# The last stage of tiles 0 to 11 beside the last expert blocks of layer 1, in a two-layer graph-attention and mixture-of-experts kernel

## The chip, the cores and the metric

The kernel runs on one core of one Trainium2 chip. Times are device microseconds (us) of one execution. A profile records one further execution: its span runs from the first to the last recorded instruction of the program.

## What is computed

Two layers over 2708 tokens of 256 float32 numbers, each layer a graph attention and a mixture of experts with two experts per token. The part that the change touches is the end of layer 1:

```python
x = x + _L1_gnn_ref(_layernorm(x), adj, 1, ...)        # attention; its result is the x below
x = x + _L1_ffn_ref(_layernorm(x), gate_w, ..., gamma, beta)

def _L1_ffn_ref(x, gate_w, gate_b, w1, b1, w2, b2, gamma, beta):   # x: (2708, 256), E = 16, K = 2
    topk_vals, topk_idx = jax.lax.top_k(x @ gate_w + gate_b, K)
    topk_w = jax.nn.softmax(topk_vals, axis=-1)
    h = jax.nn.relu(jnp.einsum('bsh,ehf->bsef', x, w1) + b1)
    expert_out = jnp.einsum('bsef,efh->bseh', h, w2) + b2
    sel = jnp.take_along_axis(expert_out, topk_idx[:, :, :, None], axis=2)
    y = x + jnp.sum(topk_w[..., None] * sel, axis=2)
    mu, var = jnp.mean(y, axis=-1, keepdims=True), jnp.var(y, axis=-1, keepdims=True)
    return (y - mu) / jnp.sqrt(var + EPS) * gamma + beta
```

For every token, y is the normalised row plus two weighted expert outputs. y is normalised once more, scaled by gamma, shifted by beta, and added to the residual x.

## The kernel before

Tokens lie in 22 tiles: 20 of 128 rows and two of 74 (`TAIL`). The attention of layer 1 hands over groups of six tiles (the last of four). For each group a router picks two experts per token and writes the token's row twice into a DRAM table, `rows_d`, ordered so that each 128 rows (a block) belong to one expert. Blocks are made known in three stages: blocks 0 to 7 after 12 tiles, 8 to 19 after 18 tiles, the rest after all. 45 blocks always run (`SURE1`); more run only if a number read at run time says so (`rest`, L926 to L929, which every engine passes).

`Experts.stream` runs the blocks. For block b:

- SP fetches the block's 128 rows (`fetch`, L759), and loads the expert's weights w1 (`load_w1`, L743) and w2 (`load_w2`, L747), 512 KB each, into one of three rooms. Each weight load carries a condition: it is skipped when block b - 3, which used the same room, had the same expert.
- PE turns the rows (L455), ACT copies them (L992). PE computes the hidden layer in four pieces (L874), ACT applies the relu (L878), PE the outputs (L889, L892).
- DVE makes `side` (L866), ACT from it the weight w (L868), DVE finishes w (L896) and scales the outputs into `yo` (L898, four buffers).
- POOL issues an indirect DMA that adds the 128 rows of `yo` to one of two DRAM tables, `sums1[b % 2]` (`add`, L903). Two adds to the same table wait for each other's landing; `sums1[0]` also holds the normalised rows, so that the two tables together give y.

The outputs of block b - 1 come behind the hidden layer of block b on PE.

PE, ACT, DVE and SP run their instructions in the order in which the program issues them. That order is made by a planner, `Clock`: every piece of work is a generator that names an engine and a planned time, or waits for a mark; the planner resumes whichever is due first, and the instructions are issued then. A hidden piece is planned at 0.47 us, a turn at 0.4, a block's outputs at 2.05, handing over between engines at 0.25, a fetch at 0.5 us of DMA and 2.2 of latency, each weight load at 1.7 and 2.0. Lower `urgency` numbers go first. The order of POOL's instructions is not written by hand: whatever is ready in the build's own plan is placed first. Each engine, SP's queue of DMAs included, takes its instructions strictly in order.

Beside the stream, `add_beta(b)` is called once for every block. From block 22 on it issues two POOL operations for one tile (L1854, L1855), which turn x1, the residual, into x1 + common + beta.

After the stream comes the last stage, `last1`, for all 22 tiles in groups of 2, 2, 4, 4, 4, 4, 2 (`firsts`). `load_y` issues two loads per group, one from each table, into `y_all` (L1444, L1447; `y_all` lies in memory that held the attention mask). For each pair of tiles PE adds the two tables' rows into a PSUM bank, by multiplying with the identity (L1894), and DVE takes the statistics (L421, L422). For each group ACT computes the reciprocal root (L428, L429), DVE mends it by one Newton step and makes the shift (L374). Then ACT scales the rows (L446), POOL multiplies by gamma (L1914), DVE adds x1 (L1918, L1924) and SP stores pairs of tiles (L1920, L1926). The loads must wait until all 45 adds have landed; they follow on POOL a closing step of the conditional part.

Of the kernel before, what the change touches and what calls it, by code (L numbers as in the profile page):

```python
# [17 lines left out]
OP = mybir.AluOpType  # L18
# [4 lines left out]
P = 128  # L23
# [123 lines left out]
def kernel(  # L147
# [559 lines left out]
    class Experts:  # L707
# [5 lines left out]
        def __init__(self, layer, router, w1, b1, w2, func, sums, tags, xg, xt, bias, sure):  # L713
            self.layer, self.router, self.w1, self.w2 = layer, router, w1, w2
            self.func, self.sums, self.b1 = func, sums, b1
            self.t_tag, self.h_tag, self.o_tag = tags
            self.xg_tile, self.xt_tile, self.bias_tile = xg, xt, bias
            E, _, self.F = w1.shape
            self.FC, self.NB = self.F // P, router.blocks
            self.rooms, self.rows, self.known, self.planned, self.stages = {}, {}, 0, 0, []  # L720
            self.last_add, self.adds = {}, []
            self.b1_rows = w1x.rearrange("p c f -> p (c f)")[:E, :self.F]
            self.taken, self.sure = taken_of[layer], sure

# [176 lines left out]
        def add(self, b, yo):  # L901
            k = b % 2
            ins = nc.gpsimd.indirect_dma_start(  # L903
                out=self.sums[k][:, :], in_=yo, in_offset=None,
                out_offset=bass.IndirectOffsetOnAxis(ap=self.rows.pop(b)[:, D:D + 1].bitcast(I32),
                                                     axis=0), compute_op=OP.add)
            if k in self.last_add:
                tc.add_manual_dep(ins.ins, self.last_add[k].name, LANDED, reason="the same rows")
            self.last_add[k] = ins.ins
            if k == 0:  # L910
                self.adds.append(ins.ins)

        def outputs(self, b, ht, w):
            ps = ps_tile("out_ps", self.o_tag)
# [3 lines left out]
        def store(self, t, r, src):  # L918

            ins = nc.sync.dma_start(self.sums[0][t * P:t * P + r, :], src)  # L920
            for other in self.adds:
                tc.declare_no_dep(ins.ins, other, reason="other tokens' rows")

        def rest(self):

# [10 lines left out]
        def stream(self, clock, stages, bank, acc, xrs, los, wides, widened, started):  # L936

            NB, FC = self.sure, self.FC
            self.known_at, self.planned_at, self.scattered_at = (
                {upto: Mark() for upto in stages} for _ in range(3))  # L940
            hidden_at, out_at, xg_at, xt_at, ht_at, w_at = (
                [Mark() for _ in range(NB)] for _ in range(6))
            xr_slots, xts, weights, hidden = {}, {}, {}, {}
# [5 lines left out]
            def fetcher():  # L949
                for b in range(NB):  # L950
# [4 lines left out]
                    xr_slots[b] = yield from xrs.get()  # L955
                    self.fetch(b)
                    clock.moved(xg_at[b], 0.5, 2.2)

            def loader():
                yield widened  # L960
                for b in range(NB):
# [14 lines left out]
                        yield out_at[b - 3]  # L976
                    self.load_w2(b)
                    clock.moved(w_at[b], 1.7, 2.0)

            def turn(b):  # L980
                yield xg_at[b]
# [27 lines left out]
            def finish(b, ps, slot):  # L1009
                yield "DVE", 0.7  # L1010
                yo = self.scaled(b, ps, weights.pop(b))
                clock.set(slot)
                yield "POOL", 1.6
                self.add(b, yo)
                clock.set(xr_slots.pop(b))

            def outputs(b):
                slot = yield from acc.get()
# [420 lines left out]
    def fetch_rows(tl, src, group):  # L1439

        full = [t for t, r in group if r == P]
        if full:
            lo = full[0] * P
            nc.sync.dma_start(tl[:, :len(full)], src[lo:lo + len(full) * P, :].rearrange(  # L1444
                "(t p) d -> p t d", p=P))
        if len(full) < len(group):
            nc.sync.dma_start(tl[:TAIL, len(full):], src[TF * P:W, :].rearrange(  # L1447
                "(t p) d -> p t d", p=P)[:TAIL])

    x_d = dram.tile([W, D], F32, name="x_d")  # L1450

# [394 lines left out]
        experts1.add_room(2, room[:, :1024], room[:, 1024:])  # L1846

    def add_beta(b):
        if b == 20:
            for name, src in (("gamma", L1_ffn_gamma), ("beta", L1_ffn_beta)):  # L1850
                last[name] = broadcast_rows(name, src, 0, D, nc.sync, last["pool"])
        if 22 <= b < 22 + T:
            t, r = tiles[b - 22]
            nc.gpsimd.tensor_scalar(x1[:r, t, :], x1[:r, t, :], common[:r, t:t + 1], None, op0=OP.add)  # L1854
            nc.gpsimd.tensor_tensor(x1[:r, t, :], x1[:r, t, :], last["beta"][:r], OP.add)  # L1855

    experts1.beside = add_beta
    for t in range(2):
        clock.start(finish1(*tiles[t]), 0)
    clock.start(widener())  # L1860
    clock.start(attention(), 2)
    experts1.stream(clock, (*early1.values(), experts1.NB), bank, acc, xrs, los, wides, widened,
                    started)
    clock.run()
    experts1.rest()
    experts1_scope.close()

    psum_stage(wide=5, acc=3)

    y_all = mask_flat.bitcast(F32)[:, :2 * T * D].rearrange(  # L1870
        "p (k t d) -> p k t d", k=2, d=D)
    clock = Clock()
    bank = Slots(clock, 5)

    def load_y(group, mark):
        lo = group[0][0]
# [34 lines left out]
    def out_rows(pair):  # L1911
# [9 lines left out]
        else:  # L1921
# [3 lines left out]
            t = pair[0][0]  # L1925
            nc.sync.dma_start(of_pair(out, t, TAIL), y_all[:TAIL, 1, t:t + 2])  # L1926

    nc.scalar.preload_act_table_set(LN_TABLE)
    loads = [Mark() for _ in firsts]
    for group, mark in zip(firsts, loads):  # L1930
        load_y(group, mark)
    for group, mark in zip(firsts, loads):
        clock.start(last1(group, mark))
    clock.run()

# [30 lines left out]
```

## Time and profile before

| | us |
|---|---|
| median of 4 runs (lowest, highest) | 1169.46 (1167.52, 1173.39) |
| profiled execution: its own time | 1166.51 |
| its span | 1164.8 |
| mean granted TensorE clock | 0.952 |
| add of block 44 (the last) starts | 1113.03 |
| first load of the last stage is issued | 1118.66 |
| last DVE operation (L1918) starts | 1157.81 |
| last output is issued | 1158.53 |

Over the span PE is busy 1052.9 us, DVE 527.2, ACT 586.4 and POOL 404.9. Busy times are averages over very different stages, so the prediction reads the stretch around the change and the wait that ends last in it. In the profile's lines, L12 is line 12 of the kernel, `out<-in` names the tiles written and read, xN counts instructions, and [a <-b] is the idle time before the instruction and what ended it. SPq marks the issue of a DMA on SP's queue, not its transfer. PEld is the loading of matmul weights.

### The profile page before, as it was taken

To read this page: it belongs to the slowest core of one execution; us is meant where nothing else is said; L and a number is where in the kernel's file an instruction comes from. 1 tells how busy PE (TensorE), PEld (TensorE's weight loads), DVE (VectorE), ACT (ScalarE), POOL (GpSimd) and SP (SyncE) were. 2 spreads that over 40 slices of the span, in tenths; PEclk is the share of its full clock that TensorE was granted. 3 is DMA by queue.
4 is the path that set the end of the run, shared out by engine and by line. 5 is a ranking of instruction groups with operands and counts; after the bars stand their busy time and mean duration, and the time that the engine had idled before them with its cause. 6 is when DMAs were issued, how large, how long until landed. Compare 5 with 4: busy or idle time off the path is not lost. (4 is left out here: it accounts for less than half of the span.)

```text
span 1164.8 us, 21436 instructions
## 1 busy us (share of the span) xinstructions
PE 1052.9 (90%) x6753; PEld 933.5 (80%) x6753; DVE 527.2 (45%) x2024; ACT 586.4 (50%) x1637; POOL 404.9 (35%) x467
## 2 busy tenths in 40 slices
PE   5999999987999999999999859998985899999963
PEld 3788888876789999998999824898985788889852
DVE  7778888866431111111001164747778551111136
ACT  4876666654434444443444347527744544444413
POOL 7621121111142222221222261253555375484325
PEclk9999999998999999999999979999887799999987
DMA  9954445310888999999899589400224477878963
GB/s 299 311 206 154 163 154 176 136 77 31 295 274 279 326 322 322 319 293 345 258 309 324 163 271 262 159 1 8 75 82 137 124 211 185 196 197 208 250 195 107
DMA packets 163486, 238.96 MB, mean 205 GB/s; under 512 B 10415, under 2 KB 137046, under 8 KB 160658
## 3 DMA queue, kind: packets, MB, share of 16 engines
q1 hardware_dynamic: 144550, 214.09, 55.1%
q0 software_dynamic: 18816, 23.42, 10.5%
q8 instruction: 57, 0.93, 0.3%
q14 instruction: 63, 0.52, 0.1%
HBM read 205.54 MB, written 54.99 MB: 224 GB/s over the span
## 5 line engine op out<-in xcount | busy, mean ns | idle before, releaser
L898 DVE TENSOR_SCALAR yo<-out_ps,w 128x256 f32<-128x256 f32 x92 | 44.5, 484 | 421.8 <-PE out_ps L892 421.6
L1219 PE MATMUL att_ps<-g_all,z 128*128 128x257 f32 (+3 forms) x968 | 227.5, 388 | 0.0
L1219 PEld LDWEIGHTS att_ps<-g_all,z 128*128 128x128 f32 (+3 forms) x968 | 177.6, 189 | 36.2 <-issue 8.8
L892 PE MATMUL out_ps<-room,ht 128*128 128x256 f32 x872 | 201.7, 383 | 0.0
L892 PEld LDWEIGHTS out_ps<-room,ht 128*128 128x128 f32 x872 | 163.0, 193 | 21.4
L874 PEld LDWEIGHTS hid_ps<-xt,room 128*128 128x128 f32 x1504 | 174.9, 192 | 3.0 <-ACT xt L859 0.8
L874 PE MATMUL hid_ps<-xt,room 128*128 128x128 f32 x1504 | 175.9, 275 | 0.5 <-ACT xt L859 0.5
L1205 ACT ACTIVATE zr<-e_bc,minus_one,g_all 128x256 f32<-128x256 f32 (+3 forms) x242 | 130.7, 591 | 55.1 <-DVE z L1208 54.4
L903 POOL DMA_INDIRECT sums<-yo,xg x43 | 66.9, 1557 | 245.0 <-DVE side L866 208.1
L878 ACT ACTIVATE ht<-hid_ps,w_t 128x128 f32<-128x128 f32 x376 | 128.2, 364 | 22.9 <-PE hid_ps L874 3.5
L668 POOL DMA_INDIRECT rows_d<-xr,place x88 | 92.0, 1045 | 125.3 <-DVE xr L437 77.0
L1570 PE MATMUL att_ps<-half,wide_mask 128*128 128x258 f32 (+1 forms) x968 | 127.2, 294 | 2.4 <-ACT h_all L1507 1.5
L1570 PEld LDWEIGHTS att_ps<-half,wide_mask 128*128 128x128 f32 (+1 forms) x968 | 124.0, 198 | 3.8 <-ACT h_all L1507 2.4
L1208 DVE SCALAR_TENSOR_TENSOR z<-zr,mask_t 128x256 f32<-128x256 f32 (+3 forms) x242 | 98.3, 427 | 34.6 <-ACT zr L1205 18.0
L878 ACT ACTIVATE ht<-hid_ps,w1x 128x128 f32<-128x128 f32 x180 | 65.1, 364 | 92.7 <-PE hid_ps L874 88.2
L868 ACT ACTIVATE w<-xg,side 128x1 f32<-128x1 f32 x43 | 12.7, 295 | 167.6 <-DVE side L866 167.6
L903 POOL DMA_INDIRECT sums<-yo,xr x45 | 70.1, 1557 | 77.0 <-DMA sums<-yo,xr 26.5
L455 PE MATMUL tr_ps<-ident,xr 128*128 128x128 f32 (+1 forms) x222 | 42.2, 302 | 34.3 <-DMA h_all<-sums 13.6
L1430 POOL CAST wide_mask<-mask_t 128x1408 fp32r<-128x1408 fp8e4 x31 | 42.5, 1378 | 83.1 <-PE att_ps L1570 83.1
L874 PE MATMUL hid_ps<-lo,wide_mask 128*128 128x128 f32 x480 | 64.6, 290 | 4.8 <-DMA wide_mask<-in_L_ffn_w_dram 4.6
L874 PEld LDWEIGHTS hid_ps<-lo,wide_mask 128*128 128x128 f32 x480 | 61.6, 204 | 8.7 <-issue 7.8
L455 PEld LDWEIGHTS tr_ps<-ident,xr 128*128 128x128 f32 (+1 forms) x222 | 30.3, 158 | 42.5 <-issue 17.2
(287 smaller groups left out, 1430.7 us busy)
## 6 DMA issues: line engine op xcount, KB each, us to landing
room<-in_L_ffn_W_dram SPq DMA_DIRECT2D x94, 1024.0 KB
wide_mask<-in_L_ffn_w_dram SPq DMA_DIRECT2D x60, 512.0 KB
room<-in_adj_dram SPq DMA_DIRECT2D x20, 1354.0 KB
room<-in_L_ffn_w_dram SPq DMA_DIRECT2D x30, 512.0 KB
rows_d<-nobody SPq DMA_DIRECT2D x1, 7511.0 KB
rows_d<-nobody SPq DMA_DIRECT2D x5, 1295.0 KB
sums<-nobody SPq DMA_DIRECT2D x2, 2944.0 KB
xr<-rows_d SPq DMA_DIRECT2D x45, 129.5 KB
```

The source lines that it names most:

```text
L455: nc.tensor.transpose(ps[:, c, :r], src[:, c * P:(c + 1) * P], ident[:r, :r])
L668: ins = nc.gpsimd.indirect_dma_start(out=self.rows_d[:, :], in_=self.rows[t][:r], in_offset=None, out_offset=bass.IndirectOffsetOnAxis(ap= ...
L874: nc.tensor.matmul(ps[:, :P], w1_b[:, c, f * P:(f + 1) * P], xt[:, c, :], start=(c == 0), stop=(c == DC - 1))
L878: nc.scalar.activation(ht[:, f, :], ps[:, :P], self.func, bias=self.bias[:, f, b:b + 1])
L892: nc.tensor.matmul(ps[:, :D], ht[:, f, :], self.rooms[b % 3][1][:, f, :], start=False, stop=(f == self.FC - 1))
L898: nc.vector.tensor_scalar(yo, ps[:, :D], w, None, op0=OP.mult)
L903: ins = nc.gpsimd.indirect_dma_start(out=self.sums[k][:, :], in_=yo, in_offset=None, out_offset=bass.IndirectOffsetOnAxis(ap=self.rows.pop ...
L1205: nc.scalar.activation(zr[:k, :n], e_bc[:k, lo:lo + n], AF.Relu, bias=minus_one[:k], scale=g_all[:k, j, D + 1:D + 2])
L1208: nc.vector.scalar_tensor_tensor(z[:k, :n], zr[:k, :n], 1.0, mask_t[:k, j // 2, lo:lo + n, j % 2], op0=OP.add, op1=OP.mult)
L1219: nc.tensor.matmul(accs[i][:r, :D + 1], z[:k, q * P:q * P + r], g_all[:k, j, :D + 1], start=(j == 0), stop=(j == LAST))
L1430: nc.gpsimd.tensor_copy(m, src)
L1570: nc.tensor.matmul(accs[i][:, :D + 2], wide_masks[i, j % 2][:k, j // 2, :], half_k[:k, j, :], start=(j == 0 and half_k is halves[0]), stop ...
```

## The change

Tiles 0 to 11 leave the last stage. They are handled in two groups of six, as pieces of the planner's run that also holds the stream:

- Tiles 0 to 5 (group 0) are read once block 35's add is planned to have landed, tiles 6 to 11 (group 1) once block 38's is, and all weights and fetches have been issued. Each group takes two DMAs, one per table, for all six tiles. `early_read` declares a read free of the adds of later blocks, and `add` declares later adds free of the reads.
- In place of PE's identity products, POOL sums the two tables' rows in pairs of tiles (128x512), and DVE takes the statistics from SBUF. In place of ACT's root, DVE computes it for the group with an integer start and three Newton steps (13 small operations). In place of ACT's scaling, POOL's product and DVE's sum, DVE runs two `scalar_tensor_tensor` per tile.
- Group 0's outputs are stored behind all weights and fetches; group 1's behind the late loads.
- The residual's two POOL operations become one DVE operation per tile (`add_to_x`), from block 20 on; gamma and beta are fetched at block 16 instead of 20.
- The last stage keeps tiles 12 to 21, in groups of 2, 2, 4 and 2.

```diff
@@ class Experts: add, store
-            if k == 0:
-                self.adds.append(ins.ins)
+            for other in self.early_reads[k]:
+                tc.declare_no_dep(ins.ins, other, reason="other tokens' rows")
+            self.adds[k].append((b, ins.ins))
...
+        def early_read(self, k, ins, done):
+            for b, other in self.adds[k]:
+                if b >= done:
+                    tc.declare_no_dep(ins.ins, other, reason="other tokens' rows")
+            self.early_reads[k].append(ins.ins)
@@ stream: fetcher, loader, finish
+                clock.set(self.fetched)
...
+                clock.set(self.loaded)
...
                 self.add(b, yo)
                 clock.set(xr_slots.pop(b))
+                clock.set(self.added_at[b], 4.5)
@@ beside the stream
     def add_beta(b):
-        if b == 20:
+        if b == 16:
...
-        if 22 <= b < 22 + T:
-            t, r = tiles[b - 22]
-            nc.gpsimd.tensor_scalar(x1[:r, t, :], x1[:r, t, :], common[:r, t:t + 1], None, op0=OP.add)
-            nc.gpsimd.tensor_tensor(x1[:r, t, :], x1[:r, t, :], last["beta"][:r], OP.add)
+        if 20 <= b < 20 + T:
+            clock.start(add_to_x(*tiles[b - 20]), 3)
+
+    def add_to_x(t, r):
+        yield "DVE", 0.47
+        nc.vector.scalar_tensor_tensor(x1[:r, t, :], x1[:r, t, :], common[:r, t:t + 1],
+                                       last["beta"][:r], op0=OP.add, op1=OP.add)
...
+    EARLY_LAST = ((tiles[:6], 36), (tiles[6:12], 39))
+    def early_last(group, done):
+        yield experts1.added_at[done - 1]
+        mark, lo, n = Mark(), group[0][0], len(group)
+        if lo:
+            yield experts1.loaded
+            yield experts1.fetched
+        for k in range(2):
+            experts1.early_read(k, fetch_rows(y_all[:, k, lo:lo + n], sums1[k], group), done)
+        clock.moved(mark, 0.8 * n, 2.5)
+        yield mark
+        for t in range(lo, lo + n, 2):
+            yield "POOL", 1.3
+            nc.gpsimd.tensor_tensor(y_all[:, 0, t:t + 2], y_all[:, 0, t:t + 2],
+                                    y_all[:, 1, t:t + 2], OP.add)
+        for t, r in group:
+            yield "DVE", 0.63
+            ln_y.stats(y_all[:, 0, t], t, r)
+        yield small(13)
+        rsqrt(ts(ln_y.mv[:, lo:lo + n, 1], LN_EPS, OP.add), ln_y.rstd[:, lo:lo + n])
+        for t, r in group:
+            yield "DVE", 0.95
+            y = y_all[:, 1, t]
+            nc.vector.scalar_tensor_tensor(y, y_all[:, 0, t], ln_y.mv[:, t, 0:1], last["gamma"],
+                                           op0=OP.subtract, op1=OP.mult)
+            nc.vector.scalar_tensor_tensor(y, y, ln_y.rstd[:, t:t + 1], x1[:, t, :], op0=OP.mult,
+                                           op1=OP.add)
+        if not lo:
+            yield experts1.loaded
+            yield experts1.fetched
+            early_out(group)
+
+    def early_out(group):
+        for (t, _), _ in zip(group[::2], group[1::2]):
+            nc.sync.dma_start(of_pair(out, t), y_all[:, 1, t:t + 2])
@@ before the stream's run, and behind it
+    for group, done in EARLY_LAST:
+        clock.start(early_last(group, done), 4)
     clock.run()
...
-    for group, mark in zip(firsts, loads):
+    late_last = [tiles[12:14], tiles[14:16], tiles[16:20], tiles[20:22]]
+    for group, mark in zip(late_last, loads):
         load_y(group, mark)
-    for group, mark in zip(firsts, loads):
+    early_out(tiles[6:12])
+    for group, mark in zip(late_last, loads):
         clock.start(last1(group, mark))
```

## The prediction

> **What bounds the kernel now.** First the chain of waits, from its end: the last 46.1 us of the span are the last stage, and it begins with a wait for the adds of layer 1's expert blocks.
>
> ```profile
> 1091.34 27.25 DMA sums<-yo,xr x3
> ...
> 1118.66 0.39 SPq L1444
> ...
> 1122.24 9.16 DMA mask_t<-sums
> ...
> 1131.44 5.03 PE y_ps L1894 x22
> ...
> 1157.81 0.69 DVE mask_t L1918
> ```
>
> Read: start, length, what. The first load of the last stage (L1444) goes out at 1118.66, when the last add has landed; rows keep arriving until 1131.4; then DVE and POOL work through 22 tiles until 1158.5, and the span ends at 1164.8. Next the busy times by stretch of time (us; busy us and instructions of PE, weight loads, DVE, ACT, POOL; granted clock; DMA share, GB/s).
>
> ```profile
> 1086.00:1090.50 4.50, 4.50 (x33) 4.20 (x32) 0.67 (x3) 1.82 (x6) 1.54 (x1) 1.00 0.76 170
> 1090.50:1103.00 12.50, 12.13 (x85) 10.82 (x84) 2.39 (x10) 5.46 (x18) 4.64 (x3) 1.00 0.99 293
> 1103.00:1109.00 6.00, 6.00 (x47) 5.71 (x46) 0.94 (x6) 3.36 (x11) 2.98 (x2) 1.00 0.34 52
> ```
>
> During the last blocks PE is never idle for long, DVE is busy a fifth of the time; and the DMA engines are full from 1090.5 to 1103, with room on both sides. In the same view the last stage, 1125 to 1165, has DVE busy for 28.0 of 40 us. So the change takes work from a stretch that DVE's and POOL's queues set, and lays it where PE sets the pace with 3.84 us a block (hidden layers start at 1086.54, 1090.38, 1094.22).
>
> **What goes (gain 15.0 us).** Only 10 of 22 tiles stay behind the last add. I lay them on the rows of before, counted from the first load's issue. First rows: +2.8 (1121.47). A pair takes 8 matmuls, 0.43 us apart while the clock is at half (the granted clock is 0.66 over 1113 to 1125), then 0.22. Tiles 12-13 end at +6.3, 14-15 at +9.2, 16-17 start at +9.8, where the third load's tiles started in before (1128.44), and end at +11.6; 20-21 end at +13.3, 18-19 at +15.1 (the plan sends the second pair of a group of four behind the next group's first). Their statistics (0.6 a tile) end at +16.4. From there to the last DVE add before took 9.7 us (1148.8 to 1158.5). Of this the bare chain is 7.0: root 0.5, five small DVE operations 1.0, the first scaling 0.65, four POOL products 0.72 to 1.17 each (4.1), the add 0.7. The rest was other groups' work in the same queues. Ends 7.0 and 9.7, I take the middle, 8.4: +24.8. The last output takes 6.3 (1158.53 to 1164.8): +31.1 against 46.1. Gain 15.0, from 13.7 to 16.4.
>
> **First early read (cost 2.3).** Where it stands on SP follows from the plan. Block 35's add counts as landed 7.3 us after its outputs' matmuls (0.25 + 0.7 + 0.25 + 1.6 + 4.5). One planned block is 4 x 0.47 + 0.63 + 2.05 = 4.56, so 7.3 lies after the first quarter of block 38's hidden layer (5.03, where w1 of block 40 is issued) and before the end of block 37's outputs (9.1, w2 of 40). Counting back from the last w1, block 44 at 1100.24, that is between these rows of SP:
>
> ```profile
> 1085.24 0.09 SPq L743 DMA_DIRECT2D wide_mask<-in_L_ffn_w_dram  x1
> 1086.73 0.08 SPq L747 DMA_DIRECT2D wide_mask<-in_L_ffn_w_dram  x1
> 1087.66 0.36 SPq L759 DMA_DIRECT2D xr<-rows_d  x1
> 1089.52 0.39 SPq L743 DMA_DIRECT2D room<-in_L_ffn_w_dram  x1
> ```
>
> The 0.08 us issues are skipped loads (same expert as three blocks before; few bytes move after them), the 0.37 us ones real. Block 40 is skipped, 41 to 43 are loaded. SP hardly waits for the add: add 35 starts at 1078.60, and adds land 3.6 to 6.1 us after their start, by 1084.7. Two reads at about 0.5 us of issue fit before 1086.73, where SP waits for PE's outputs anyway. What is late next is the weights queued behind 1.57 MB (2 x 6 tiles x 128 KiB). From 1086 to 1090.5 the engines moved 0.77 MB; the full slices of the last stage's loads show 347 GB/s, or 1.56 MB in 4.5 us. So 0.79 MB finds room and 0.78 MB, 2.3 us, pushes the full stretch. Nothing there gives it back: block 42's hidden layer waited 0.26 us for w1 already. Ends 0 (all hidden) and 4.5 (nothing hidden).
>
> **DVE's own order (cost 0.5).** DVE runs group 0's statistics at a written place, planned 11.7 us after the read. If rows come later, the next block's `side` waits, ACT's `w` behind it, the relus behind that, and PE. The rows: 2.8 for the first pair's landing plus 1.2 MB at 347 makes about 6.5, and three sums on POOL (groups of instructions: count, shapes, busy us, mean ns; POOL over the span, DVE from 855 to 975):
>
> ```profile
> L1468 POOL TENSOR_TENSOR h_all<-h_all,xp 128x512 f32<-128x512 f32 x10 | 11.9, 1191 | 3.1 <-DMA xp<-sums 3.1
> ...
> L1778 DVE SCALAR_TENSOR_TENSOR h_all<-h_all,common,xp 128x256 f32<-128x256 f32 x8 | 3.7, 465 | 0.0
> ...
> L421 DVE BATCH_NORM_STATS2 bn<-h_all 128x6 f32<-128x256 f32 x8 | 3.4, 428 | 0.3
> ```
>
> 3 x 1.19 = 3.6, so all is there after 10.1, or 12.0 with an add (1.55 + 0.3) between. The planned 11.7 are 2.1 to 2.6 real blocks of 3.84, 8 to 10 us. So up to 2 us late, but PE is 2.3 late then from its weights. Ends 0 and 2; I take 0.5. A group's DVE work is 6 x 0.61 statistics, 13 small x 0.165 and 12 x 0.465, 11.4 us; with `add_to_x`, 0.47 a block, it lies beside PE, as DVE has some 3 us free in each block.
>
> **Second read (cost 2.2).** It goes out behind w2 of block 44 (1102.60), where the DMA engines are 0.34 busy, and lands by 1109.1 to 1109.5. Then three sums, 3.6 us, stand in POOL's queue among the last adds:
>
> ```profile
> 1107.56 1.55 POOL L903 DMA_INDIRECT sums<-yo,xr  x1 [2.65 <-DVE w L896]
> 1111.18 1.54 POOL L903 DMA_INDIRECT sums<-yo,xr  x1 [2.08 <-DMA sums<-yo,xr]
> 1113.03 1.55 POOL L903 DMA_INDIRECT sums<-yo,xr  x1 [0.31 <-DVE yo L898]
> ```
>
> Blocks 42, 43, 44. POOL's order is not written by hand. Sums ahead of add 43 end at 1113.1, add 43 starts at 1113.4, 44 at 1115.25: 2.2 late, and the late loads with it. Sums ahead of 42: it starts at 1113.4, and 44 must wait for its landing (3.9): 4.4 late. Sums behind 44 hold only POOL's closing step before the loads (1117.04): 1.2, or 0.5 if one sum fits before add 43. I take 2.2, ends 0.5 and 4.4. DVE's 11.4 us then run from 1111 to 1122.5, ahead of the first late statistics (1125.3): nothing, with the end at 1.5 if the sums come last. The early outputs (2 x 0.79 MB) go behind all loads: nothing.
>
> **POOL's 44 operations (L1854, L1855) that go:** no wait of PE names them; 17 in a row held add 21 for 12.6 us (1018.47 to 1031.06), and PE went on. Nothing, with up to 1 us of gain, since one small DVE operation took 1.22 instead of 0.16 beside them.
>
> [...] Beside POOL's products, DVE's add of 128x512 took 0.69 at the median and 1.21 at most, POOL's product 0.72 and 1.83 at most. [...]
>
> **Sum:** 15.0 - 2.3 - 0.5 - 2.2 = 10.0. The profiled execution ran 1166.51 (span 1164.8 and 1.7 around it): 1156.5. The median of the runs, 1169.46, is 2.95 above it, so **1159.5** on the runs' scale. About 0.5% (5.8 us) is what a measurement of this kernel can tell from no change.
>
> **Rivals** (runs' scale).
> - *Nothing hidden* (0.16): the first read meets loaded blocks (4.5), DVE waits 2, the sums stand before add 42 (4.4), the end gives 13.7: gain 2.8, 1166.7. For it: 0.99 busy from 1090.5. Against: the skipped block 40.
> - *SP stands* (0.08), slower: SP takes its queue in order, and the first read waits for add 35. If POOL runs that add late, weights 41 to 44 wait with it, us for us, and pay back nothing in a full stretch. It decides from a lag of 10.0 us. The trace's longest hold of an add, 12.6, with three sums ahead, 3.6, gives 16.2: 6.2 slower, 1175.7. Against: what made that hold is removed, and adds 30 to 40 start 0.3 us after `yo`.
> - *It doesn't come loose* (0.08): the second read still waits for all adds. Then 11 of group 1's DVE us lie in the end: 15.0 - 2.8 - 11 = 1.2, 1168.3. Against: each later add is declared free of it.
> - *All hidden* (0.10): gain 16.4 - 0.5 = 15.9, 1153.6.
> - *Forecast* (0.58), its own range 1155.5 to 1163.5.
>
> Faster: 0.58 + 0.10 + 0.04 of the first rival = 0.72; same: 0.12 + 0.08 = 0.20; slower 0.08. The range 1153.0 to 1167.5 takes in the ends of the costs and leaves out the two rivals above it, 0.16.
>
> **What would show it.** Right: first late load about 5 us later than 1118.66, and some 31 us from it to the end; two 768 KiB reads between w1 and w2 of block 40; hidden layer 41 or 42 waits some 2 us for weights; POOL's sums just ahead of the last adds. Wrong: SP idle before the first read; DVE idle before the statistics with PE idle too; over 34 us behind the late loads.

## The result, and the profile after

The changed kernel takes 1165.39 us (median; 1159.47 to 1170.54), the kernel before in more runs 1169.42 (1162.78 to 1177.94). The ratio is 0.9964, with a 95% interval from 0.9954 to 0.9974: about 4.2 us faster, where 10.0 were forecast. The profiled execution of the changed kernel ran 1166.67 (span 1164.7, clock 0.948), so it shows no gain over the one of before; single executions spread by more than the gain. So stretches are compared within one execution, and whole times by ratios.

The table cuts the span at five events ("again" is a second profile of the changed kernel). The last two columns belong to experiments that are told below and stand here for comparison (us).

| stretch | before | after | after, again | sums on DVE | sums on DVE, 74-row reads split |
|---|---|---|---|---|---|
| start to add 0 | 918.91 | 920.12 | 915.96 | 919.33 | 916.48 |
| add 0 to add 18 | 91.38 | 95.42 | 98.09 | 95.78 | 95.52 |
| add 18 to add 35 | 68.32 | 68.62 | 67.56 | 67.52 | 68.18 |
| add 35 to PE's last output product | 33.62 | 35.04 | 35.97 | 37.27 | 37.44 |
| from there to the first late load | 6.44 | 9.32 | 9.39 | 10.03 | 9.76 |
| first late load to the end | 46.12 | 36.15 | 36.75 | 34.19 | 31.33 |

In the first two columns the changed kernel gives up 4.0, 1.4 and 2.9 us (second, fourth and fifth row) on the way to its first late load, and wins 10.0 behind it. Forecast were 0, 2.8, 2.2 and 15.0. It also loses 1.2 and 0.3 in the first and third row; the first differs by 4.2 between the two executions of the changed kernel, so its 1.2 is not read as a loss. Two rows are far off: the second, where the forecast had no term at all, and the last.

**The second row.** SP's queue beside block 18 (timeline; start, length of the issue, line, tile):

```profile
996.75 0.40 SPq L743 DMA_DIRECT2D wide_mask<-in_L_ffn_w_dram  x1
997.20 0.47 SPq L228 DMA_DIRECT2D gamma<-in_L_ffn_gamma_dram  x1
997.72 0.49 SPq L228 DMA_DIRECT2D beta<-in_L_ffn_beta_dram  x1
998.63 0.39 SPq L747 DMA_DIRECT2D wide_mask<-in_L_ffn_w_dram  x1
```

and the busy times by stretch (PE, weight loads, DVE, ACT, POOL; granted clock; DMA share, GB/s) of the same kernel:

```profile
1003.00:1006.00 3.00, 2.07 (x12) 1.49 (x9) 0.67 (x3) 0.64 (x2) 0.58 (x1) 1.00 0.93 263
1006.00:1009.00 3.00, 0.00 (x0) 0.00 (x1) 0.00 (x0) 0.00 (x0) 1.55 (x1) 1.00 1.10 330
1009.00:1012.00 3.00, 2.97 (x14) 3.00 (x15) 0.00 (x0) 1.04 (x4) 0.00 (x0) 0.52 1.07 387
```

The fetch of gamma and beta, moved from block 20 to 16, now stands between w1 and w2 of block 18, in the first of three blocks in a row that need real loads (the loads of 16 and 17 are skipped). PE stands still from 1005 to 1009, in front of hidden layer 19, and then runs at a granted clock of 0.52 (a share of full speed). The DMA share adds up the time of the packets and can pass 1 (1.10 from 1006 to 1009).

**The last row.** The end of the blocks and the start of the last stage (timeline; the bracket is the idle time before, and what ended it):

```profile
1101.58 2.02 PE L874 MATMUL hid_ps<-lo,room 128*128 128x128 f32 x16 [1.66 <-DMA room<-in_L_ffn_w_dram]
...
1108.82 2.05 POOL L903 DMA_INDIRECT sums<-yo,xr  x1 [4.17 <-DMA sums<-yo,xr]
1109.67 0.99 SPq L1457 DMA_DIRECT2D mask_t<-sums  x2
...
1123.27 1.55 POOL L903 DMA_INDIRECT sums<-yo,xr  x1 [1.32 <-SPq L937]
1124.27 4.27 POOL L1898 TENSOR_TENSOR mask_t<-mask_t 128x512 f32<-128x512 f32 x3
1126.14 0.43 DVE L421 BATCH_NORM_STATS2 bn<-mask_t 128x6 f32<-128x256 f32 x1 [6.43 <-POOL mask_t L1898]
1128.51 2.98 SPq L1457 DMA_DIRECT2D mask_t<-sums  x6
...
1138.41 10.76 PE L1940 MATMUL y_ps<-mask_t,ident 128*128 128x256 f32 x40 [19.23 <-DVEq L937]
```

Read from top to bottom: hidden layer 41 waits 1.66 us for weights, as forecast. The second read goes out at 1109.67. Group 1's three sums run at 1124.27, behind add 44 (1123.27), the last in POOL's queue; DVE has idled 6.43 us for them. The first late load goes out at 1128.51, 9.85 later than before. PE's first y product comes 9.9 us behind that load, and it waits not for rows but for DVE: L937 is the conditional that every engine passes behind the blocks, and DVE reaches it when group 1's work is done, at 1137.6. In before the same product comes 2.8 us behind the load and waits for rows:

```profile
1121.47 9.18 PE L1894 MATMUL y_ps<-mask_t,ident 128*128 128x256 f32 x26 [9.25 <-DMA mask_t<-sums]
```

The stretches that answer to the three shown of before, 5.5 us later since add 36 is 5.5 late:

```profile
1091.50:1096.00 4.50, 4.50 (x32) 4.20 (x31) 1.06 (x4) 1.76 (x6) 1.56 (x1) 1.00 1.05 311
1096.00:1108.50 12.50, 10.84 (x79) 9.92 (x78) 8.19 (x34) 5.13 (x17) 6.82 (x5) 1.00 1.09 347
1108.50:1114.50 6.00, 5.89 (x41) 5.21 (x40) 5.73 (x17) 2.44 (x8) 3.60 (x2) 1.00 0.61 192
```

The early reads filled what room there was on the DMA engines (0.76 became 1.05 in the first row), and group 0's DVE work lies beside PE as intended (8.19 and 5.73 busy for 2.39 and 0.94).

### The profile page after: what moved, and what is told of

The parts are those of the page before. It is cut to its first block, busy times and chain, and to the rows that moved or that the text cites. A ratio compares the mean times of both kernels' runs of the same rounds, so it can differ in the third digit from the quotient of the medians.

```text
span 1164.7 us, 21306 instructions
## 1 busy us (share of the span) xinstructions
PE 1040.2 (89%) x6705; PEld 922.9 (79%) x6705; DVE 540.8 (46%) x2076; ACT 578.2 (50%) x1619; POOL 368.2 (32%) x417
## 5 line engine op out<-in xcount | busy, mean ns | idle before, releaser
L1584 PE MATMUL att_ps<-half,wide_mask 128*128 128x258 f32 (+1 forms) x968 | 124.8, 290 | 2.5 <-ACT h_all L1521 1.5
L1221 DVE SCALAR_TENSOR_TENSOR z<-zr,mask_t 128x256 f32<-128x256 f32 (+3 forms) x242 | 98.1, 427 | 33.0 <-ACT zr L1218 17.9
L878 ACT ACTIVATE ht<-hid_ps,w1x 128x128 f32<-128x128 f32 x180 | 62.0, 362 | 92.4 <-PE hid_ps L874 89.6
```

The source lines that it names most:

```text
L878: nc.scalar.activation(ht[:, f, :], ps[:, :P], self.func, bias=self.bias[:, f, b:b + 1])
L1221: nc.vector.scalar_tensor_tensor(z[:k, :n], zr[:k, :n], 1.0, mask_t[:k, j // 2, lo:lo + n, j % 2], op0=OP.add, op1=OP.mult)
L1584: nc.tensor.matmul(accs[i][:, :D + 2], wide_masks[i, j % 2][:k, j // 2, :], half_k[:k, j, :], start=(j == 0 and half_k is halves[0]), stop ...
```

## The experiments

Theory: four separate losses. (A) gamma and beta ahead of real weight loads; (B) group 1's DVE work lies in the end, since its sums stand last on POOL; (C) the second read slows the last adds; (D) something in the late stage itself, open at first. Rivals: the stores compete with the adds; PE's half clock (granted 0.50 from 1138.4 to 1142 in the changed kernel) sets the end; the end is bound by something else and (B) is hidden.

Ratios are to runs of the kernel before on the same chip on the same occasion. It took 1196 us on the first and third occasions and 1170 on the second and fourth, so times of different occasions are not set against each other.

### Where gamma and beta are fetched (A)

In the changed kernel:

```diff
-        if b == 16:
+        if b == 19:
             for name, src in (("gamma", L1_ffn_gamma), ("beta", L1_ffn_beta)):
```

> The changed kernel, with the two broadcast loads of gamma and beta issued at block 19 instead of 16; nothing else moves, on any engine. They then stand beside w1 of block 21, which is skipped, instead of w2 of block 18, which is loaded. Theory A: the 3.96 us that PE waits at block 18's successor, and most of the 5.5 us by which the changed kernel is late at add 35, come from these two loads standing in a full stretch of DMA. Then the wait falls under 1 us, add 35 comes within 1.5 us of 1078.6, and the time drops by 4 to 5.5 us (ratio to the changed kernel about 0.996). Rival B: the stall is a chance of that one execution; then the median moves under 1 us. Rival C: DVE's new operation per block makes the stream late; then add 35 stays some 5 us late.

And the reverse, in the kernel before:

```diff
-        if b == 20:
+        if b == 16:
```

> The kernel before, with the two broadcast loads of gamma and beta issued at block 16 instead of 20, and nothing else. Theory A: the same stall appears here alone, some 4 us at the hidden layer of block 18 or 19, and the time rises by 4 to 5.5 us to about 1174. Rivals B and C: no change.

Measured: ratios 0.9955 [0.9935, 0.9974] and 1.0057 [1.0036, 1.0078]. The kernel before with the fetch at 16 has the wait, and slow products behind it (16 in 3.75 us instead of 2.02; in the changed kernel they took 3.65, at the granted clock of 0.52); in the changed kernel with the fetch at 19 PE waits 0.78 us there. Both rows are PE's hidden layer 19 (some expectations call it 18), of before with 16 and of the changed kernel with 19:

```profile
1042.16 3.75 PE L874 MATMUL hid_ps<-lo,wide_mask 128*128 128x128 f32 x16 [3.02 <-DMA wide_mask<-in_L_ffn_w_dram]
```

```profile
1027.44 2.02 PE L874 MATMUL hid_ps<-lo,wide_mask 128*128 128x128 f32 x16 [0.78 <-DMA wide_mask<-in_L_ffn_w_dram]
```

On the first and third occasions add 0 to add 18 took 102.5 and 103.4 us with 19, 105.6 to 108.8 with 16 (five executions of variants of the changed kernel); in the other executions, of the kind in which before takes 1170, 90.6 and 91.0 against 95.4 to 98.1 (six). So (A) is shown in this stretch, at 2 to 7 us an execution. Whole times show it clearly in the kernel before alone (6.8 us slower, 4.3 to 9.3). In the changed kernel they do not: its ratio with 19, 0.9955, lies 1 us under its ratio with 16, 0.9964, where the expectation had 4 to 5.5, and the intervals overlap.

256 KB at the 347 GB/s of the last stage's loads in before would be 0.75 us, a fifth of the wait. The bytes are not the price: in the changed kernel the DMA engines have a share of 0.30 and move 65 GB/s from 1000 to 1002, although w2 of block 18 was issued at 998.63; in before, from 999 to 1001, it is 0.92 and 277. Why the engines stand nearly idle behind this fetch is open.

### Group 0's stores behind the late loads

```diff
-        if not lo:
-            yield experts1.loaded
-            yield experts1.fetched
-            early_out(group)
...
+    early_out(tiles[:6])
     early_out(tiles[6:12])
```

> The changed kernel with the three stores of tiles 0 to 5 issued behind the late loads instead of behind the second early read. Theory D: the landings of adds 40 and 41, 8.7 and 7.9 us against 3.7 to 4.0 before, are slow because the second read and these stores fill the DMA engines, and adds 42 to 44 wait for them (the last add 3 us later than PE's end explains). Then without the stores adds 41 and 42 land 1 to 3 us sooner, the last add starts within 1.5 us of its scaled row, and the time drops by 1 to 3 us, unless what follows waits for DVE in any case (theory E), when it drops under 1. Rival F: POOL's sums, not the landings, hold the adds; then nothing changes.

Measured: 0.9982 [0.996, 1.0004]. The adds keep their pattern (40 at 1132.69, 42 at 1142.33, 44 at 1146.81: 9.6 and 4.5 apart, 9.4 and 5.1 in the changed kernel), the first late load is 9.1 us behind PE's last output. The stores do not slow the adds; that rival falls.

### Group 1's DVE work behind the conditional (B)

```diff
+    def early_sum(group, mark):          # the sums and all DVE work, taken out of early_last
...
-    early_out(tiles[6:12])
+    there = Mark()
+    there.at = 0.0
+    clock.start(early_sum(tiles[6:12], there), 0)
```

> The changed kernel with group 1's DVE work (statistics, root, two operations per tile) issued behind the conditional part instead of ahead of it; the read and POOL's sums stay where they are. Theory E: PE's first product of the last stage came 9.9 us after the first late load instead of 2.8, because PE waits there for DVE to have passed the conditional part, and DVE had 11 us of group 1's work in its queue ahead of it. Then PE starts 2.5 to 3.5 us after the first late load, DVE ends the same work, and the time drops by 3 to 5 us. Rival G: the late rows themselves came late (the queue, or the stores of tiles 0 to 5); then PE starts as late as in the changed kernel, and the time stays within 1 us.

Measured: 0.9993 [0.9966, 1.002]. The edit puts the three sums behind the conditional too, where the expectation leaves them; they run behind add 44 (1146.91) as in the changed kernel. PE is free of DVE's passing of the conditional, and its first y product comes 2.85 us behind the first late load:

```profile
1147.91 4.26 POOL L1906 TENSOR_TENSOR mask_t<-mask_t 128x512 f32<-128x512 f32 x3
1149.78 0.43 DVE L421 BATCH_NORM_STATS2 bn<-mask_t 128x6 f32<-128x256 f32 x1 [5.85 <-POOL mask_t L1906]
...
1152.31 3.04 SPq L1457 DMA_DIRECT2D mask_t<-sums  x6
...
1155.16 6.45 PE L1946 MATMUL y_ps<-mask_t,ident 128*128 128x256 f32 x18 [11.75 <-DMA mask_t<-sums]
```

But the end is no nearer, where 3 to 5 us were expected: 36.7 us from that load. The sums still come behind add 44, DVE starts at 1149.78 and reaches the first late statistics at 1161.2, 8.9 us behind the load. What PE no longer waits for, DVE's queue now holds. So the wait at the conditional is real and is only the face of the loss; the loss is when group 1's sums are made.

### The changed kernel again, and group 1's sums on DVE (B)

> The changed kernel again, on the chip of the other three runs, so that they can be compared with it. Ratio to the kernel before 0.9964 as measured, 0.995 to 0.998. Both theories: the first y product some 9.9 us behind the first late load, 36.2 us from that load to the end of the span.

Measured: 0.9967 [0.9937, 0.9998]; first y product 9.7 us behind the load, 36.75 to the end.

```diff
         for t in range(lo, lo + n, 2):
-            yield "POOL", 1.3
-            nc.gpsimd.tensor_tensor(y_all[:, 0, t:t + 2], y_all[:, 0, t:t + 2],
-                                    y_all[:, 1, t:t + 2], OP.add)
+            yield "DVE" if lo else "POOL", 1.3
+            (nc.vector if lo else nc.gpsimd).tensor_tensor(
+                y_all[:, 0, t:t + 2], y_all[:, 0, t:t + 2], y_all[:, 1, t:t + 2], OP.add)
```

> Group 1's three sums on DVE instead of POOL; no other instruction changes its engine. In the changed kernel they stand on POOL behind add 44 (1124.27), and DVE idles 6.43 us for them with the rows there. Theory (group 1's DVE work lies in the end because its sums stand last on POOL): 3 x 0.7 = 2.1 us on DVE from 1119.7, statistics from about 1121 instead of 1126.1, DVE through group 1 by 1132 to 1133, the first y product 4 to 5 us behind the first late load instead of 9.9, 31 to 32 us from that load to the end instead of 36.2; ratio to the changed kernel 0.996. Rival (the late tiles' loads or PE's cold clock set the end, DVE's place does not count): the first y product comes earlier, the end stays at 36 us; ratio 1.000.

Measured: 0.9958 [0.9938, 0.9978].

```profile
1110.76 0.99 SPq L1457 DMA_DIRECT2D mask_t<-sums  x2
...
1119.72 1.29 DVE L1898 TENSOR_TENSOR mask_t<-mask_t 128x512 f32<-128x512 f32 x2 [1.14 <-DMA mask_t<-sums]
...
1129.93 3.04 SPq L1457 DMA_DIRECT2D mask_t<-sums  x6
...
1134.23 8.14 PE L1940 MATMUL y_ps<-mask_t,ident 128*128 128x256 f32 x26 [14.32 <-DVEq L937]
...
1144.29 4.93 PE L1940 MATMUL y_ps<-mask_t,ident 74*74 74x256 f32 x14 [1.93 <-DMA mask_t<-sums]
```

The first y product comes 4.3 us behind the load instead of 9.9, as the theory has it; the end gains only 2 (34.2, expected 31 to 32), too little for the ratios to tell the two kernels apart. Two new waits show. The sums meet rows that land 9.0 us after their read's issue (the forecast gave 6.5 to 6.9), and `yo` 44 waits behind them. And PE, once started, runs dry: the rows of tile 20 arrive 14.4 us behind the first late load. That is (D).

### Group 0 alone early (C)

```diff
-    EARLY_LAST = ((tiles[:6], 36), (tiles[6:12], 39))
+    EARLY_LAST = ((tiles[:6], 36),)
...
-    late_last = [tiles[12:14], tiles[14:16], tiles[16:20], tiles[20:22]]
+    late_last = [tiles[6:8], tiles[8:10], tiles[10:12], tiles[12:16], tiles[16:20], tiles[20:22]]
...
-    early_out(tiles[6:12])
```

> Only tiles 0 to 5 early; tiles 6 to 11 go back behind the last add, loaded and worked as in the kernel before. Theory (the second read slows the landings of adds 40 and 41 from under 4 us to 8.7 and 7.9, and add 42 waits for 40): without it adds 41 to 44 land in about 4 us, add 44 starts within 1 us of PE's last output instead of 4.1, the first late load is 3 us earlier, the first y product 2.8 us behind it; from the load to the end some 38.5 us (46.1 less half of 15), so ratio to the changed kernel 1.000, to before 0.996. Rival (the three sums of group 0 or the weights slow the adds): adds 40 and 41 still land in 8 us, the load no earlier, ratio to the changed kernel 1.002 to 1.004.

Measured: 0.9984 [0.9962, 1.0006]. Without the second read the adds land sooner. DMA issues between 1105 and 1150 (count, median us from issue to landing), of the changed kernel and of this one:

```profile
sums<-yo,xr POOLq DMA_INDIRECT x5, 7.9
```

```profile
sums<-yo,xr POOLq DMA_INDIRECT x6, 4.2
```

In before it is 3.9. From PE's last output to the first late load it takes 7.3 us, against 9.3 to 9.4 with the second read and 6.4 in before. So (C) is 2.0 of the 2.9 us, less than the theory's 3; the other 0.9 came with group 0 alone. For that part the trace shows a way: `yo` of block 42 starts 2.5 us after PE's last product for it (1113.72 and 1116.20; in before 0.04 us), behind group 0's operations on DVE; add 42 is as late, and add 44, which waits for its landing, starts 1.45 us after its own `yo` instead of 0.28. No run takes this delay out by itself. The end was mis-sized again: 41.35 us for 16 tiles, expected 38.5.

### All sums on DVE, gamma and beta at 19

The edit above without its condition (`"DVE", 0.7` and `nc.vector` for both groups), and `b == 19`.

> The sums of both groups on DVE, and gamma and beta fetched beside block 19 instead of 16. Theory (three separate losses: 3.96 us of PE waiting behind the gamma and beta fetch, about 5 us of group 1's DVE work in the end, 2.4 us of add 39 behind group 0's sums): ratio to the changed kernel 0.990 to 0.993, to before 0.987 to 0.990; the first y product 4 to 5 us behind the first late load. Rival (DVE, with group 0's sums ahead of a block's side, holds PE up instead): PE waits of 1 us or more for DVE or ACT at hidden layers 41 or 42, ratio to the changed kernel 0.995 or above.

Measured: 0.994 [0.9913, 0.9966]. (A)'s 5 us are won, but some of it is lost again: DVE now idles 1.84 us in front of group 0's sums (1094.37) with the next `side` behind them, hidden layer 41 waits 2.61 us, and add 35 to PE's last output takes 38.1 us. The rival is partly right.

### The 74-row reads first (D)

The reads of tiles 20 and 21 (L1460) go out ahead of the other late loads; PE keeps its order. Alone, then with group 1's sums on DVE, then with gamma and beta at 19 as well:

```diff
-    for group, mark in zip(late_last, loads):
+    for k in range(2):
+        fetch_rows(y_all[:, k, 20:22], sums1[k], late_last[3])
+    for group, mark in zip(late_last[:3], loads):
         load_y(group, mark)
+    clock.moved(loads[3], 0.8 * 2, 2.0)
```

> The changed kernel with one shift in SP's order: the two reads of tiles 20 and 21 (74 rows each, L1460) go out ahead of the late loads of tiles 12 to 19, not behind them; PE keeps its order. In the changed kernel PE starts its y products only when DVE is through (9.9 us behind the first late load), and then meets no wait for rows. Theory (DVE's order sets the end in this kernel, the slow 74-row reads lie hidden behind it): nothing, ratio to the changed kernel 0.999 to 1.001, 35.5 to 36.5 us from the first late load to the end. Rival (the landing of the 74-row reads sets it): 3 us or more off the end, ratio 0.997.

> Group 1's sums on DVE and the 74-row reads first; gamma and beta stay beside block 16. Against the run with the sums on DVE alone (34.2 us from the first late load to the end; PE waited 1.93 us for the rows of tile 20, 14.4 us behind the first late load). Theory (the 74-row reads, which move some 49 GB/s, are the next bound once DVE's order is eased): no such wait, PE's last y product some 15 to 16 us behind the first late load instead of 19.3, 30 to 32 us to the end, ratio to the kernel before 0.992 to 0.994. Rival (PE's half clock alone makes the products late): the last product still at 19 us, 34 us to the end, ratio 0.996.

> Three edits together: gamma and beta fetched beside block 19; group 1's sums on DVE (group 0's stay on POOL); the 74-row reads of tiles 20 and 21 ahead of the other late loads. Theory (the losses are separate): the wait of 3 to 4 us at hidden layer 18 goes, the first y product stands 4 to 5 us behind the first late load, no wait of PE for rows of tiles 20 and 21 (1.9 us, with its matmuls then at half clock, in the run with the sums on DVE), 30 to 32 us from the load to the end; span some 9 us under the changed kernel's, ratio to the kernel before 0.987 to 0.990. Rival (a later bound takes the gain of the last edit): 34 us from the load to the end as without it, ratio 0.992.

Measured: 0.9984 [0.9958, 1.001], 0.9999 [0.9978, 1.0019] and 0.9944 [0.991, 0.9977]; 37.0, 36.0 and 36.9 us from the first late load to the end. The second and third are misses. The first alone:

```profile
1156.73 0.81 SPq L1460 DMA_DIRECT2D mask_t<-sums  x2
1157.60 7.13 SPq L1457 DMA_DIRECT2D mask_t<-sums  x6
...
1167.73 10.52 PE L1940 MATMUL y_ps<-mask_t,ident 128*128 128x256 f32 x40 [20.17 <-DMA mask_t<-sums]
```

PE now waits for rows of tile 12 until 11 us behind the load (9.9 and 10.6 in the others) although DVE is through before. So the 148 KB reads held up what stood behind them; the six issues took 7.13 us, and 2.98 in the changed kernel. How slow they are shows in a stretch where nothing else moves, of the kernel before (its 74-row reads, hidden there behind 12 more tiles of work) and of the run with the sums on DVE, while PE waits for tile 20 (the last two numbers are DMA share and GB/s):

```profile
1139.50:1142.00 2.50, 2.50 (x12) 2.21 (x13) 2.40 (x5) 0.96 (x3) 2.32 (x4) 1.00 0.14 48
```

```profile
1142.00:1144.00 2.00, 0.36 (x2) 0.00 (x0) 1.69 (x9) 1.86 (x4) 1.21 (x2) 1.00 0.14 49
```

0.14 of 16 engines is 2.2: by an estimate from these rows about two engines carry the reads, at some 24 GB/s each, and the 296 KB of both reads take 6 us. The full slices of before's last stage show 347 GB/s. Why 74 rows are slow is not shown, and that 64 and 10 would be faster no run had shown by then.

### The 74-row reads split (D)

```diff
         for k in range(2):
-            fetch_rows(y_all[:, k, lo:lo + len(group)], sums1[k], group)
+            if lo < TF:
+                fetch_rows(y_all[:, k, lo:lo + len(group)], sums1[k], group)
+                continue
+            for p0, p1 in ((0, 64), (64, TAIL)):
+                nc.sync.dma_start(y_all[p0:p1, k, lo:], sums1[k][TF * P:W, :].rearrange(
+                    "(t p) d -> p t d", p=P)[p0:p1])
```

With group 1's sums on DVE; the same with gamma and beta at 19; and the split alone:

> Group 1's sums on DVE, and each late read of tiles 20 and 21 (74 rows) as two reads, of 64 and of 10 rows; gamma and beta beside block 16. While only the 74-row reads move, the DMA share is 0.13 at 47 GB/s in the kernel before and 0.14 at 49 GB/s in the run with the sums on DVE, that is two of the 16 engines, and there PE waited for the rows of tile 20 until 14.4 us behind the first late load; with these reads first, all other rows came behind them and PE began only 9.9 to 11 us behind the load. Theory (the 74-row read on two engines is the bound that the forecast of the end left out): split, it lands 3 to 4 us earlier, PE's last y product stands 16 us behind the first late load instead of 19.3, the end 31 us instead of 34.2; ratio to the kernel before 0.992 to 0.994. Rival (the stores and the half clock set the end): 34 us, last product at 19, ratio 0.996.

> The same with gamma and beta fetched beside block 19 instead of 16: the version that the runs so far point to. Theory (separate losses add up): 4 to 5 us less than the run before this one up to block 18, the same end; ratio to the kernel before 0.987 to 0.990. Rival (what the early blocks gain is lost again to the early reads): 0.993 or above.

> The changed kernel with only the 74-row reads split in 64 and 10 rows. There PE's y products start 9.9 us behind the first late load and then wait for no rows. Theory (in the changed kernel DVE's group 1 work sets the end, the 74-row reads are hidden): no change of more than 1 us, 35.5 to 36.5 us from the first late load to the end, ratio to the kernel before 0.995 to 0.998. Rival (the slow reads hold the end as well): 34 us or less.

Measured: 0.9908 [0.9879, 0.9938], **0.9882** [0.9854, 0.9909] and 0.9971 [0.995, 0.9992]. The first and the second:

```profile
1127.37 3.01 SPq L1457 DMA_DIRECT2D mask_t<-sums  x6
1130.43 2.59 SPq L1928 DMA_DIRECT2D mask_t<-sums  x4
1132.74 10.48 PE L1945 MATMUL y_ps<-mask_t,ident 128*128 128x256 f32 x40 [15.12 <-DVEq L937]
...
1151.92 0.69 DVE L1969 TENSOR_TENSOR mask_t<-mask_t,h_all 128x512 f32<-128x512 f32 x1 [0.62 <-POOL mask_t L1965]
```

```profile
1124.91 3.04 SPq L1457 DMA_DIRECT2D mask_t<-sums  x6
1127.99 3.31 SPq L1928 DMA_DIRECT2D mask_t<-sums  x4
1129.52 11.24 PE L1945 MATMUL y_ps<-mask_t,ident 128*128 128x256 f32 x40 [14.51 <-DVEq L937]
```

All 40 products in one run, the last 15.8 us behind the load (19.3 without the split), and 31.33 and 31.35 us from the load to the end. In the first the DMA engines move 316 GB/s from 1134 to 1137 and nothing from 1140 to 1143, so all rows are there 12.6 us behind the load, where those of tile 20 took 14.4. No run shows the reads of 64 and of 10 rows apart. Alone the split does nothing (37.4 us to the end, ratio as the changed kernel's): there DVE's order hides it. So (B) and (D) are one behind the other; each alone pays 2 us or nothing, both together 5. With the split in place, taking the sums off POOL is worth 6.0 us behind the late load, and 6.3 in whole time on the same occasion (1160.84 against 1167.18). The half clock is not what held the end at 34 to 37: PE still starts its products at a granted clock of 0.50 (1131 to 1134) in the kernel that ends at 31.33. The second kernel, 1158.1 against 1170.5, is the fastest of all: 0.9882 / 0.9964 puts it 0.8% under the changed one. Against the first it gains 4.5 us from add 0 to add 18, but 2.7 in the median, where 4 to 5 were expected, and the two intervals overlap.

### Both reads behind all weights

```diff
-        if lo:
-            yield experts1.loaded
-            yield experts1.fetched
+        yield experts1.loaded
+        yield experts1.fetched
```

> The changed kernel with the first early read behind all weights too (both groups read there). It measures the price of the first read on PE by itself: from the start of add 35 to PE's last out product the kernel before took 33.6 us, the changed kernel 35.1 to 37. Theory (the first read costs PE 2 to 3 us of weight waits): 33.6 to 34, no wait over 1 us at hidden layers 41 to 43. Rival (the DVE work of group 0 or its sums slow PE): 35 or more with the read gone. In both, DVE's work of both groups (23 us) now lies behind the last add, the first y product some 20 us behind the first late load, and the end some 10 us later than the changed kernel's.

One execution: 1204.0 us, beside 1195.6 for the kernel before. Add 35 to PE's last output takes 33.9 us (before 33.6; six runs of the first and third occasions with the first read among the weights 34.8 to 37.4). So the first read costs PE 1 to 3.5 us, together with group 0's sums and DVE work, which the edit moves out of this stretch as well. In the changed kernel PE's waits in this stretch are for weights (0.96 us ahead of the read, 1.66 behind it). The end was not as expected: group 0's stores go out at 1160.45, when DVE is through with that group, and the late loads, behind them on SP, at 1169.04, 25.6 us behind PE's last output.

## Why the prediction was wrong, step by step

- **"What goes (gain 15.0 us)" is the main step that failed:** 10.0 were measured. The chain of late tiles was laid on the rows of before as if nothing but DVE, PE and ACT could hold it. "First rows: +2.8" became +9.9 for PE's first product, behind DVE's group 1 work (next point), and "Their statistics (0.6 a tile) end at +16.4" became +22.5. Hidden behind that lay a second error, "20-21 end at +13.3": their rows alone arrive at +14.4, from a read that moves at 49 GB/s (DMA share 0.14), which in before had 12 more tiles of work to hide behind. With that read split and group 1's sums out of POOL's queue the stretch is 31.33 us, where the forecast had 31.1. Two things that hold the chain were missed: the sums, 2.0 to 2.6, and behind them the read, 2.9. That the rest agrees to 0.2 us is partly luck: in that run the statistics end at +17.6, 1.2 late, and the way from there to the end is 13.7 us instead of 14.7.
- **"Second read (cost 2.2)... DVE's 11.4 us then run from 1111 to 1122.5": failed in its mechanism.** The sums did not stand among the last adds, they came last; DVE ran from 1126.1 to 1137.7. That case had been priced "the end at 1.5 if the sums come last"; the first y product came 7.1 us later than in before, and the end 2.0 to 2.6, or 6.0 with the 74-row reads split. That the read "lands by 1109.1 to 1109.5", 6.5 to 6.9 us after its issue, was short too: in the run with the sums on DVE the rows took 9.0. The cost ahead of the late loads, 2.9, was near 2.2, but by luck: it came from adds that landed in 8 us beside a 1.57 MB read, and in part from late `yo` rows, not from sums in their way.
- **Gamma and beta moved from block 20 to 16: no term at all,** and 4.0 us in the profiled execution. It was the smallest line of the diff. The issues of 0.07 and 0.4 us on SP could have told: the loads of 16 and 17 are skipped, those of 18 to 20 are not, and the fetch stands in the first of these.
- **"First early read (cost 2.3)": right.** The two reads stand between w1 and w2 of block 40 at 1090.92, SP did not wait, hidden layer 41 waited 1.66 us; 1.4 us in this execution, 1 to 3.5 over the runs.
- **"DVE's own order (cost 0.5)": another path.** The forecast led it over `side` to PE, and no PE wait in the changed kernel is put down to it. But `yo` of block 40 starts 2.4 us after its last product (1105.66 and 1108.05; in before 0.04), behind group 0's statistics and root, and the chain of adds 40, 42 and 44 begins with it. The 0.9 us of the run with group 0 alone is the nearest that a run comes to its price.
- **POOL's 44 operations** gone: nothing seen. **Early outputs:** nothing, shown for group 0's.
- **Signs.** Right: the reads' place, the wait of hidden layer 41. Wrong: the first late load 9.85 later and not 5, and "over 34 us behind the late loads", which was named as a sign against, is what came (36.15).
- **The rivals.** "It doesn't come loose" had "11 of group 1's DVE us lie in the end": the second read did come loose, but DVE's work lay there all the same, for another reason and at a fifth of the price (half of it once the 74-row reads are split). "SP stands" did not happen. "Nothing hidden" is nearest in time (1166.7), but none of its conditions came: the first read cost 1.4 and not 4.5, PE waited 0 and not 2 for DVE, none of group 1's sums stood before add 42, and the end gave 10.0 and not 13.7.

The sum, with measured terms: 10.0 - 1.4 - 2.9 - 4.0 = 1.7, and less the 1.2 and 0.3 of the first and third row 0.1, which is the difference of the two spans. The medians say 4.2. A difference of that size between two executions is not resolved by one profile each, and how the 5.8 us between forecast and medians divide among the steps stays open to that extent. That 1165.39 still lies between 1153.0 and 1167.5 is luck: what failed is not among the costs whose ends made that range.

DVE beside POOL's sums: of the changed kernel's 46 DVE operations with two SBUF inputs (L1871, L1908, L1910), 45 took 0.47 to 0.49 us, most of them beside an add's issue; one stood beside POOL's sums:

```profile
1099.22 3.71 POOL L1898 TENSOR_TENSOR mask_t<-mask_t 128x512 f32<-128x512 f32 x3 [0.79 <-DMA mask_t<-sums]
...
1102.22 0.99 DVE L1871 SCALAR_TENSOR_TENSOR h_all<-h_all,common,beta 74x256 f32<-74x256 f32 x1
```

It ends 0.28 us after the third sum (1102.93), and the same operation does so in the 12 other profiles in which it meets these sums on POOL (0.99 to 1.01 us each). It cost 0.5 us on DVE here; what that is at the end is not shown.

## What to carry to other kernels

When most of a stage is taken away, look at what that stage was hiding, slow transfers above all: look for stretches in which the DMA share is a small fraction of the 16 engines, and ask when the last byte lands once the work in front of it is gone. Work that is laid beside other work must also be released there: find the last instruction that it waits for in the queue of its producer, since a planned place on DVE is worth little if the sums stand last on POOL. And price every moved DMA, the smallest too, against what is queued behind it at its new place.

## What the runs showed of the hardware that was not expected

- Reads of 74 rows, alone on the DMA engines, moved 48 to 49 GB/s at a DMA share of 0.14. Put first, they held up the reads of 128 rows behind them: PE's first rows came 9.9 to 11 us behind the first issue instead of 2.8 in before.
- Indirect adds of 128 rows took 3.9 us from issue to landing in the last blocks of before and 5.9 to 6.1 beside weight loads (adds 34 to 36), but 8.7 and 7.9 beside a 1.57 MB read of the tables that they add to (adds 40 and 41). Whether the tables or only the full DMA engines matter is not shown.
- Two fetches of one 1 KB row into 128 partitions each, 256 KB in all, in front of three blocks' weight loads cost PE 2.6 to 4.3 us of waiting for weights (12 executions with the fetch at 16); behind the wait 16 products took 2.0 to 3.8 us, without a wait 1.95.
